# Attention on one core: the order and the step size in which the SP queue brings queries, masks and the last stage's inputs

## The chip, the cores and the metric

The kernel runs on one core of a Trainium2 chip. A core has a matrix engine (PE), a vector engine (DVE), an activation engine (ACT), a general engine (POOL), and a sequencer (SP) that in this kernel issues the DMA transfers. Each engine has its own instruction stream and runs it in order; streams meet at semaphores. The metric is the device time of one execution in microseconds (us), less is better. It is the median of several runs.

## The reference, cut to what matters

Two graph attention layers and one transformer layer over 4096 nodes with 256 features, all sharing one 4096 x 4096 adjacency matrix. The change lies in the transformer layer. It has 8 heads of 32 features each:

```
qkv = layer_norm(x, g1, be1) @ w_qkv
q, k, v = split of qkv into 8 heads of 32
scores = (q . k) * 32**-0.5           # 8 x 4096 x 4096
scores = where(adj != 0, scores, -inf)
attn = softmax(scores)
x = x + (attn @ v) @ w_proj + b_proj
x = x + gelu(layer_norm(x, g2, be2) @ w1 + b1) @ w2 + b2
```

## The kernel before, in words

The graph attention layers and the query, key and value products of the transformer come first and are not touched. Then `unshifted_transformer` (L1633) runs the attention stage and the last stage (projection, layer norm, two feed-forward products).

**The attention stage.** Queries are cut into 8 blocks of 512 (`nb`), heads into two quads of four (`c`), keys into 32 tiles of 128 (`mt`). One `(nb, c, mt)` is a unit; there are 512 units, and each is done in two halves (`u`), each for two heads. `weights` (L1810) does a half: eight PE matmuls (L1819) write scores into a PSUM tile `u_ps` of 128 x 1024 numbers (three such buffers), ACT takes the exponential in place (L1826), DVE multiplies by the mask into `u_e` (L1828). PE later multiplies `u_e` with the values (`weigh`, tile `u_av`) and sums it with a column of ones (`total`, tile `u_dn`), both by `four` (L1834). For seven pairs of units out of eight, POOL adds two `u_e` first (`u_both`, L1946), so that PE sums one tile and not two; the eighth pair (`alone`, L1856) is summed tile by tile. These PE pieces wait in a list and are put behind the scores of later halves, three or four per half. At the end of a quad ACT copies both sums out (L1853, L1870), they are stored to DRAM, and two late steps reload and invert the sums (`quad_end`, L1867).

**What has to be loaded.** A block needs its queries (`u_q`, four transfers of 256 KB, L1711; two buffers) and its mask (`u_mask`, four chunks of 512 KB for eight key tiles each, L1723; five buffers). Keys and values of all tiles stay in SBUF. `load_early` (L1887) brings, in quad 1 of the last block, all weights of the last stage (`wp`, `bp`, `b2`, `w1`, `w2`) and the rows, attention sums and inverted sums of its first two blocks, into space of the keys of quad 0 (`u_k0`, no longer used by then), one `u_q` buffer and one mask buffer: some 5.5 MB. POOL adds the bias to those rows and multiplies the sums with the inverses (L1960, L1963).

**What sets the order.** Inside the attention stage PE, ACT and DVE keep the order of the program text (`manual_schedule`, L1931 and L1932). SP and POOL are not in that set: the planner of the framework places their instructions when, by its own reckoning, inputs and buffers are ready. So transfers go out when a buffer comes free and not where the text has them. In the stage before (query, key and value products) SP does keep the order of the text, and there too `load_queries(0)` and `load_chunk(0, ..)` are called. In the last stage only PE keeps the order of the text. Order between engines is kept by semaphores in every case.

Of the kernel before, what the change touches and what calls it, by code (L numbers as in the profile page):

```python
# [8 lines left out]
F32 = mybir.dt.float32  # L9
BF = mybir.dt.bfloat16  # L10
F16 = mybir.dt.float16
# [3 lines left out]
U8 = mybir.dt.uint8  # L15
# [7 lines left out]
P = 128  # L23
# [695 lines left out]
def spread(src, ap):  # L719

    return bass.AP(tensor=src.tensor, offset=src.offset, ap=ap)
# [9 lines left out]
class Rows:  # L731
# [5 lines left out]
    def load(self, to, at, cols=slice(None)):  # L737

        end = at + to.shape[1]
        for block, start, n in zip(self.blocks, block_starts(self.tiles), self.tiles):  # L740
            a, b = max(at, start), min(end, start + n)
            if a < b:
                self.nc.sync.dma_start(
                    to[:, a - at : b - at, :],
                    block[(a - start) * P : (b - start) * P, cols].rearrange(
                        "(t p) d -> p t d", p=P
                    ),
                )
# [884 lines left out]
def unshifted_transformer(  # L1633
# [22 lines left out]
    nc = tc.nc  # L1656
    N, D = out.shape
    DC = D // P
    F = w1.shape[1]
    FC = F // P  # L1660
    NT = N // P
    NB = 512
    NNB = N // NB
# [21 lines left out]
    masks = ctx.enter_context(tc.tile_pool(name="u_masks", bufs=5))  # L1685


    def load_rows(nb, res, att, inv):
        rows.load(res, nb * TB)
        nc.sync.dma_start(att, att_d[:, :, nb * NB : (nb + 1) * NB].rearrange("c p n -> p c n"))  # L1690
        for j in range(HC):
            nc.sync.dma_start(
                inv[j * O : (j + 1) * O],
                spread(inv_d[nb * DC, j : j + 1, :], [[0, O], [HC * NB, DC], [1, NB]]),
            )

    with ExitStack() as scope:
# [7 lines left out]
        def stack(to, i, order, cols, c, heads):  # L1705

            for a, kind in enumerate(order):
                if kind is None:
                    continue
                first = half_d[i, kind, c, 0:1, cols]  # L1710
                nc.sync.dma_start(  # L1711
                    to[a * O : (a + 1) * O],
                    spread(first, [[N, O], [O * N, heads], [1, NB]]),
                )

        def load_queries(nb):
            q_st = blocks.tile([P, DC * HC, NB], F16, name="u_q")
            stack(q_st, 0, (0, 1, 0, 1), slice(nb * NB, (nb + 1) * NB), 0, DC * HC)
            block_tiles[nb] = q_st, []

        def load_chunk(nb, k):
            b = masks.tile([P, MC, NB], U8, name="u_mask")
            nc.sync.dma_start(  # L1723
                b.rearrange("p (c m) n -> p c (m n)", c=2),
                mask_d[nb][2 * k : 2 * k + 2].rearrange("c p n -> p c n"),
            )
            block_tiles[nb][1].append(b)

        with ExitStack() as qkv:
            hv = qkv.enter_context(tc.tile_pool(name="u_hv", bufs=3))  # L1730
# [79 lines left out]
        def weights(nb, c, mt, u):  # L1810

            q_st, chunks = block_tiles[nb]
            mask = chunks[mt // MC][:, mt % MC, :].unsqueeze(1).to_broadcast([P, 2, NB])
            ps = ps_s.tile([P, 2, NB], F32, name="u_ps")
            for j in range(2):
                h = c * HC + 2 * u + j
                for r in range(HC):
                    at = mt * P + r * O
                    nc.tensor.matmul(  # L1819
                        ps[r * O : (r + 1) * O, j, :],  # L1820
                        k_st[c][:, 2 * u + j, at : at + O],
                        q_st[:, h, :],
                        start=True,
                        stop=True,
                    )
            nc.scalar.activation(ps, ps, AF.Exp, scale=SCALE)  # L1826
            e = work.tile([P, 2, NB], F32, name="u_e")
            nc.vector.scalar_tensor_tensor(e, mask, 0.0, ps, op0=ALU.not_equal, op1=ALU.mult)  # L1828
            return e
# [57 lines left out]
        def load_early():  # L1887

            slab = slab_p.tile([P, 32 * D], F32, name="u_k0")
            at = 0  # L1890

            def piece(n, pattern, **dims):
                nonlocal at
                at += n * D
                return slab[:, at - n * D : at].rearrange(pattern, **dims)

            early["wp"] = piece(DC, "p (c e) -> p c e", c=DC)
            nc.sync.dma_start(early["wp"], w_proj.rearrange("(c p) e -> p c e", p=P))
            for name, src in (("bp", b_proj), ("b2", b2)):
                early[name] = piece(1, "p (o e) -> p o e", o=1)  # L1900
                nc.sync.dma_start(early[name][:, 0], spread(src, [[0, P], [1, D]]))
            two = blocks.tile([P, 2, TB * D], F32, name="u_q")
            early[0] = (
                piece(TB, "p (t d) -> p t d", t=TB),
                piece(TB, "p (c n) -> p c n", c=DC),
                piece(TB, "p (c n) -> p c n", c=DC),
            )
            early[1] = (
                two[:, 0].rearrange("p (t d) -> p t d", t=TB),
                two[:, 1].rearrange("p (c n) -> p c n", c=DC),  # L1910
                masks.tile([P, DC, NB], F32, name="u_mask"),
            )
            for nb in range(2):
                load_rows(nb, *early[nb])
            early["w1"] = piece(FC, "p (c f) -> p c f", c=DC)
            nc.sync.dma_start(early["w1"], w1.rearrange("(c p) f -> p c f", p=P))
            early["w2"] = piece(FC, "p (f e) -> p f e", f=FC)
            nc.sync.dma_start(early["w2"], w2.rearrange("(c p) e -> p c e", p=P))

        early = {}  # L1920
        units = [(nb, c, mt) for nb in range(NNB) for c in range(DC) for mt in range(NT)]
# [6 lines left out]
                [lambda part=part: step(*units[i], es, part) for part in range(PARTS)]  # L1928
            )

        ordered = {mybir.EngineType.PE, mybir.EngineType.Activation, mybir.EngineType.DVE}  # L1931
        scope.enter_context(tc.manual_schedule(engines=ordered))  # L1932
        for i in range(len(units) + 5):
            for u in range(HC // 2):
                if i < len(units):
                    nb, c, mt = units[i]
                    if u == 0 and c == DC - 1 and mt % MC == 2 and nb + 1 < NNB:
                        if mt < MC:
                            load_queries(nb + 1)
                        load_chunk(nb + 1, mt // MC)  # L1940
                    if u == 0 and units[i] == (NNB - 1, DC - 1, 4):
                        load_early()
                    es_of.setdefault(i, []).append(weights(*units[i], u))
                    if i % 2 == 1 and not alone(mt):
                        both = work.tile([P, 2, NB], F32, name="u_both", bufs=6)
                        nc.gpsimd.tensor_tensor(both, es_of[i - 1][u], es_of[i][u], op=ALU.add)  # L1946
                        both_of.setdefault(i, []).append(both)
                if u == 0 and 0 <= i - 2 < len(units):
                    ready(weigh, i - 2, es_of[i - 2])
                if u == 1 and i - 4 in both_of:  # L1950
                    ready(total, i - 4, both_of.pop(i - 4))
                if u == 1 and 0 <= i - 2 < len(units) and alone(units[i - 2][2]):
                    ready(total, i - 2, es_of[i - 2])
                count = AFTER[i % 2 * 2 + u] + (len(waiting) > 3 * PARTS)
                for _ in range(min(count, len(waiting))):
                    waiting.pop(0)()
            for k, unit in enumerate(((NNB - 1, DC - 1, NT // 2 - 1), units[-1])):
                if i < len(units) and units[i] == unit:
                    res, att, inv = early[k]
                    nc.gpsimd.tensor_tensor(  # L1960
                        res, res, early["bp"].to_broadcast([P, TB, D]), op=ALU.add
                    )
                    nc.gpsimd.tensor_tensor(att, att, inv, op=ALU.mult)  # L1963
            if i == len(units) - 1:
                nc.scalar.activation(rooted, norms.eps, AF.Sqrt)
            if i % 2 == 0 and later:
                later.pop(0)()
        assert not waiting
        while later:
            later.pop(0)()  # L1970

# [1 line left out]
    with ExitStack() as scope:  # L1973
# [7 lines left out]
        def rows_of(nb):  # L1981
            res = tail.tile([P, TB, D], F32, name="u_xres", bufs=4)
            att = tail.tile([P, DC, NB], F32, name="u_att")
            inv = tail.tile([P, DC, NB], F32, name="u_wide")
            load_rows(nb, res, att, inv)
            nc.gpsimd.tensor_tensor(res, res, bp_sb, op=ALU.add)
            nc.vector.tensor_tensor(att, att, inv, op=ALU.mult)
            return res, att
# [186 lines left out]
```

## Time and profile before

| what | value |
|---|---|
| median of 3 runs | 3158.15 us (3156.18 to 3162.9) |
| the profiled execution: its own time | 3161.47 us |
| its span, first to last instruction | 3159.7 us |
| granted clock of PE over the span | 0.994 |
| attention stage, from the first scores to the last mask product | about 1700.6 to 2891.1 us |
| last stage | about 2895 us to the end |
| busy shares over the span: PE, DVE, ACT, POOL | 98%, 88%, 85%, 38% |

Times in the profile are in us from the start of the span, those of single instructions in ns where marked. An instruction group is named by its line, its engine, its operation and its tiles (out<-in). In a timeline, the bracket at the end of a line says how long the engine sat idle before it and what ended that; "issue" stands for idle time in which it waited for nothing that the profile shows. In a table of stretches, each engine has its busy time and, in brackets, its count of instructions; then follow the granted PE clock, the mean busy share of the 16 DMA engines and GB/s. DMA queues are named by number; "instruction" is the kind of the packets that bring the engines' own programs.

### The profile page before, as it was taken

To read this page: it belongs to the slowest core of one execution; us is meant where nothing else is said; L and a number is where in the kernel's file an instruction comes from. 1 tells how busy PE (TensorE), PEld (TensorE's weight loads), DVE (VectorE), ACT (ScalarE), POOL (GpSimd) and SP (SyncE) were. 2 spreads that over 40 slices of the span, in tenths; PEclk is the share of its full clock that TensorE was granted. 3 is DMA by queue.
4 is the path that set the end of the run, shared out by engine and by line. 5 is a ranking of instruction groups with operands and counts; after the bars stand their busy time and mean duration, and the time that the engine had idled before them with its cause. 6 is when DMAs were issued, how large, how long until landed. Compare 5 with 4: busy or idle time off the path is not lost. (4 is left out here: it accounts for less than half of the span.)

```text
span 3159.7 us, 138934 instructions
## 1 busy us (share of the span) xinstructions
PE 3084.4 (98%) x63976; PEld 2715.3 (86%) x63976; DVE 2786.5 (88%) x3140; ACT 2682.1 (85%) x3228; POOL 1196.6 (38%) x538
## 2 busy tenths in 40 slices
PE   6999999999999999999998999999999999999998
PEld 5899999999889999999975888888878888877766
DVE  7999999999889999999976999999999999998221
ACT  6899999999899999999965888888888888886232
POOL 3300000000320000000003988898988888997110
PEclk8999999999999999999999999999999999999999
DMA  7666554420311213121145010101011010121210
GB/s 259 220 201 197 166 190 149 151 86 23 112 44 39 79 56 96 42 67 38 46 127 158 14 41 21 34 21 34 28 27 39 18 49 8 48 61 56 70 34 22
DMA packets 212034, 250.33 MB, mean 79 GB/s; under 512 B 88241, under 2 KB 132785, under 8 KB 211441
## 3 DMA queue, kind: packets, MB, share of 16 engines
q1 hardware_dynamic: 211440, 241.36, 24.9%
q8 instruction: 502, 8.22, 1.1%
q14 instruction: 92, 0.75, 0.1%
HBM read 198.84 MB, written 42.47 MB: 76 GB/s over the span
## 5 line engine op out<-in xcount | busy, mean ns | idle before, releaser
L1462 PE MATMUL bank<-vst,t 128*128 128x132 f16 x16384 | 1457.3, 220 | 9.7 <-DVE t L1137 9.5
L1946 POOL TENSOR_TENSOR u_both<-u_e 128x1024 f32<-128x1024 f32 x448 | 1049.7, 2385 | 902.8 <-DMA u_k<-half_d 782.8
L1462 PE MATMUL bank<-vst,mask 128*128 128x132 f16 (+1 forms) x10516 | 1372.4, 206 | 0.0
L1122 ACT ACTIVATE t<-s_b,g_terms 128x1024 int8<-128x1024 f32 x1234 | 1320.8, 1162 | 24.3 <-PE bank L1462 18.9
L1462 PEld LDWEIGHTS <-t 128*128 128x128 fp8e4 x16384 | 1186.4, 96 | 22.9 <-DVE t L1137 12.5
L1828 DVE SCALAR_TENSOR_TENSOR u_e<-u_mask,u_ps 128x1024 f32<-128x1024 uint8 x1024 | 1165.9, 1220 | 23.7 <-ACT u_ps L1826 20.6
L1826 ACT ACTIVATE u_ps<-u_ps 128x1024 f32<-128x1024 f32 x1024 | 1030.0, 1008 | 147.4 <-PE u_ps L1819 49.4
L1462 PEld LDWEIGHTS <-mask 128*128 128x128 fp8e4 x10516 | 920.7, 98 | 0.0
L1137 DVE SCALAR_TENSOR_TENSOR t<-mask,t 128x2048 int32<-128x2048 int32 x256 | 588.5, 2299 | 74.8 <-ACT t L1122 66.5
L1819 PE MATMUL u_ps<-u_q,u_k 128*32 128x512 f16 x8192 | 642.6, 383 | 11.0 <-issue 7.3
L1837 PE MATMUL u_av<-u_e,u_v 128*32 128x128 f32 x16384 | 605.7, 273 | 2.6 <-issue 2.6
L1837 PEld LDWEIGHTS u_av<-u_e,u_v 128*32 128x32 f32 x16384 | 492.0, 110 | 131.5 <-issue 5.2
L1124 DVE TENSOR_SCALAR t<-s_b,g_terms 128x1024 fp8e4<-128x1024 f32 x814 | 591.0, 758 | 2.4 <-DMA s_b<-s_d 2.4
L1054 POOL TENSOR_TENSOR vst<-g_adj,vst 128x528 f16<-128x528 f32 x16 | 19.8, 1239 | 727.2 <-ACT g_big L1018 682.7
L1837 PE MATMUL u_dn<-u_both,u_ones 128*32 128x128 f32 x7168 | 281.9, 273 | 1.6 <-issue 1.6
L1819 PEld LDWEIGHTS <-u_k 128*32 128x32 f16 x8192 | 231.4, 95 | 58.6 <-issue 17.9
L1837 PEld LDWEIGHTS u_dn<-u_both,u_ones 128*32 128x32 f32 x7168 | 213.7, 110 | 41.9 <-issue 2.1
L2041 ACT ACTIVATE u_hid<-misc,n_b 128x512 f32<-128x512 f32 x64 | 43.9, 687 | 140.2 <-PE misc L2034 140.1
L2054 PE MATMUL misc<-u_k,u_hid 128*128 128x256 f32 x512 | 111.8, 379 | 0.0
L2034 PE MATMUL misc<-ln_cols,u_k 128*128 128x512 f32 x256 | 111.3, 592 | 0.5 <-ACT ln_cols L1558 0.5
L2054 PEld LDWEIGHTS misc<-u_k,u_hid 128*128 128x128 f32 x512 | 96.7, 190 | 13.3 <-issue 0.5
L2034 PEld LDWEIGHTS misc<-ln_cols,u_k 128*128 128x128 f32 x256 | 48.6, 190 | 58.5 <-issue 56.9
(171 smaller groups left out, 1808.9 us busy)
## 6 DMA issues: line engine op xcount, KB each, us to landing
g_adj<-in_adj_dram SPq DMA_DIRECT2D x123, 512.0 KB
s_b<-s_d SPq DMA_DIRECT2D x64, 512.0 KB
mask<-mask SPq DMA_DIRECT2D x128, 256.0 KB
u_mask<-mask SPq DMA_DIRECT2D x32, 512.0 KB
mask<-stage SPq DMA_DIRECT2D x48, 256.0 KB
half_d<-u_halves SPq DMA_DIRECT2D x32, 256.0 KB
u_q<-half_d SPq DMA_DIRECT2D x32, 256.0 KB
rows<-e_x SPq DMA_DIRECT2D x31, 256.0 KB
```

The costliest lines, as they stand in the source:

```text
L1122: nc.scalar.activation(to.bitcast(I8), s, AF.Sign, bias=negd, scale=-1.0)
L1124: nc.vector.tensor_scalar(to, s, negd, -1.0, op0=ALU.is_ge, op1=ALU.mult, saturate=False)
L1137: nc.vector.scalar_tensor_tensor(both, m32.unsqueeze(1).to_broadcast(list(both.shape)), SIGNS, both, op0=ALU.bitwise_or, op1=ALU.bitwise_and,)
L1462: nc.tensor.matmul(to, left, right, start=k not in opened, stop=last)
L1819: nc.tensor.matmul(ps[r * O : (r + 1) * O, j, :], k_st[c][:, 2 * u + j, at : at + O], q_st[:, h, :], start=True, stop=True,)
L1826: nc.scalar.activation(ps, ps, AF.Exp, scale=SCALE)
L1828: nc.vector.scalar_tensor_tensor(e, mask, 0.0, ps, op0=ALU.not_equal, op1=ALU.mult)
L1837: nc.tensor.matmul(to[j * O : (j + 1) * O, at], lefts[j], es[j // 2][:, j % 2, at], start=first and part == 0, stop=last and part == PARTS ...
L1946: nc.gpsimd.tensor_tensor(both, es_of[i - 1][u], es_of[i][u], op=ALU.add)
L2034: nc.tensor.matmul(ph, w1_sb[:, k, f * P : (f + 1) * P], hn[:, k, :], start=(k == 0), stop=(k == DC - 1),)
L2041: nc.scalar.activation(hid[:, f, :], ph, AF.Gelu_apprx_tanh, bias=norms.sb["b1"][:, f : f + 1])
L2054: nc.tensor.matmul(po[:, :D], hid[:, f, at : at + P], w2_sb[:, f, :], start=(f == 0), stop=(f == FC - 1),)
```

## The change

Three things change, all inside `unshifted_transformer`.

1. SP joins the set of engines that keep the order of the text in the attention stage.
2. Transfers are cut. A mask chunk of 512 KB becomes two of 256 KB. The early rows, sums and inverses go by half or by feature chunk, `w1` in four pieces of 256 KB, `wp` in two and `w2` in eight of 128 KB. Queries keep their four transfers of 256 KB.
3. A list `pacing` holds such steps. At the start of every unit `pace` takes at most one: it has ACT copy one column (`norms.eps`, 128 x 1 or 32 x 1) into the first column of the step's target, and then issues the transfer, which overwrites it. The transfer writes the same place, so it has to wait for the copy, and the copy stands in ACT's order before the unit's first exponential. The queries of block `nb + 1` enter the list at quad 0, tile 20 (four steps), the halves of mask chunk `k` at quad 1, tile `8k + 2` (two steps each), the early loads at the last block's quad 1, tile 4 (28 steps, for the 28 units that are left).

The loads of the stage before the attention (`load_queries(0)`, `load_chunk(0, ..)`) use the same steps without the copy, all at once.

```diff
+    def row_steps(nb, res, att, inv):
+        def sums(c):
+            nc.sync.dma_start(att[:, c], att_d[c, :, nb * NB : (nb + 1) * NB])
+        def inverses(c):
+            for j in range(HC):
+                nc.sync.dma_start(
+                    inv[j * O : (j + 1) * O, c],
+                    spread(inv_d[nb * DC + c, j : j + 1, :], [[0, O], [1, NB]]),
+                )
+        h = TB // 2
+        steps = [
+            (res[:, k : k + h], lambda k=k: rows.load(res[:, k : k + h], nb * TB + k))
+            for k in (0, h)
+        ]
+        for c in range(DC):
+            steps.append((att[:, c : c + 1], lambda c=c: sums(c)))
+            steps.append((inv[:, c : c + 1], lambda c=c: inverses(c)))
+        return steps
...
+        pacing = []
+        def pace():
+            if pacing:
+                (to, eps), load = pacing.pop(0)
+                nc.scalar.copy(to, eps)
+                load()
+        def query_steps(nb):
+            q_st = blocks.tile([P, DC * HC, NB], F16, name="u_q")
+            block_tiles[nb] = q_st, []
+            cols = slice(nb * NB, (nb + 1) * NB)
+            return [
+                (
+                    (q_st[a * O : (a + 1) * O, 0, :1], norms.eps[a * O : (a + 1) * O]),
+                    lambda a=a, kind=kind: stack(
+                        q_st, 0, [kind if k == a else None for k in range(HC)], cols, 0, DC * HC
+                    ),
+                )
+                for a, kind in enumerate((0, 1, 0, 1))
+            ]
...
+        def chunk_steps(nb, k):
+            b = masks.tile([P, MC, NB], U8, name="u_mask")
+            block_tiles[nb][1].append(b)
+            m = MC // 2
+            def part(c):
+                nc.sync.dma_start(
+                    b[:, m * c : m * (c + 1)].rearrange("p m n -> p (m n)"), mask_d[nb][2 * k + c]
+                )
+            return [((b[:, m * c, :1], norms.eps), lambda c=c: part(c)) for c in range(2)]
...
-            for nb in range(2):
-                load_rows(nb, *early[nb])
-            early["w1"] = piece(FC, "p (c f) -> p c f", c=DC)
-            nc.sync.dma_start(early["w1"], w1.rearrange("(c p) f -> p c f", p=P))
...
+            def add(to, load):
+                pacing.append(((to[:, 0, :1], norms.eps), load))
...
+            vector("bp", b_proj)
+            rows_of(0)
+            rows_of(1)
+            for c in range(DC):
+                matrix("wp", w_proj, c, slice(0, D))
+            for half in range(2):
+                for c in range(DC):
+                    matrix("w1", w1, c, slice(half * F // 2, (half + 1) * F // 2))
+            vector("b2", b2)
+            for f in range(FC):
+                matrix("w2", w2, f, slice(0, D))
...
-        ordered = {mybir.EngineType.PE, mybir.EngineType.Activation, mybir.EngineType.DVE}
+        ordered = {
+            mybir.EngineType.PE, mybir.EngineType.Activation, mybir.EngineType.DVE,
+            mybir.EngineType.SP,
+        }
...
-                    if u == 0 and c == DC - 1 and mt % MC == 2 and nb + 1 < NNB:
-                        if mt < MC:
-                            load_queries(nb + 1)
-                        load_chunk(nb + 1, mt // MC)
+                    if u == 0 and nb + 1 < NNB:
+                        if c == 0 and mt == 20:
+                            pacing.extend(query_steps(nb + 1))
+                        if c == DC - 1 and mt % MC == 2:
+                            pacing.extend(chunk_steps(nb + 1, mt // MC))
                     if u == 0 and units[i] == (NNB - 1, DC - 1, 4):
                         load_early()
+                    if u == 0:
+                        pace()
```

More of the change, by code (lines that the diff above doesn't have):

```diff
@@ L1714, in stack @@
                 )
-        def load_queries(nb):
-            q_st = blocks.tile([P, DC * HC, NB], F16, name="u_q")
-            stack(q_st, 0, (0, 1, 0, 1), slice(nb * NB, (nb + 1) * NB), 0, DC * HC)
-            block_tiles[nb] = q_st, []
-        def load_chunk(nb, k):
[L1722 to L1727, printed above, removed]
+        pacing = []
[17 more added lines that the diff above has]
+            ]
+        def load_queries(nb):
+            for _, load in query_steps(nb):
+                load()
+        def chunk_steps(nb, k):
[7 more added lines that the diff above has]
+            return [((b[:, m * c, :1], norms.eps), lambda c=c: part(c)) for c in range(2)]
+        def load_chunk(nb, k):
+            for _, load in chunk_steps(nb, k):
+                load()
         with ExitStack() as qkv:
@@ L1897, in load_early @@
             early["wp"] = piece(DC, "p (c e) -> p c e", c=DC)
[L1898 to L1902, printed above, removed]
+            early["bp"], early["b2"] = (piece(1, "p (o e) -> p o e", o=1) for _ in range(2))
             early[0] = (
@@ L1907, in load_early @@
             )
+            early["w1"] = piece(FC, "p (c f) -> p c f", c=DC)
+            early["w2"] = piece(FC, "p (f e) -> p f e", f=FC)
+            two = blocks.tile([P, 2, TB * D], F32, name="u_q")
             early[1] = (
@@ L1912, in load_early, with vector, rows_of, matrix @@
             )
-            for nb in range(2):
-                load_rows(nb, *early[nb])
-            early["w1"] = piece(FC, "p (c f) -> p c f", c=DC)
-            nc.sync.dma_start(early["w1"], w1.rearrange("(c p) f -> p c f", p=P))
-            early["w2"] = piece(FC, "p (f e) -> p f e", f=FC)
-            nc.sync.dma_start(early["w2"], w2.rearrange("(c p) e -> p c e", p=P))
+            def add(to, load):
+                pacing.append(((to[:, 0, :1], norms.eps), load))
+            def vector(name, src):
+                to = early[name]
+                add(to, lambda: nc.sync.dma_start(to[:, 0], spread(src, [[0, P], [1, D]])))
+            def rows_of(nb):
+                for load in row_steps(nb, *early[nb]):
+                    add(*load)
+            def matrix(name, src, c, cols):
+                to = early[name][:, c : c + 1, cols]
+                at = src[c * P : (c + 1) * P, cols]
+                add(to, lambda: nc.sync.dma_start(to[:, 0], at))
+            vector("bp", b_proj)
[9 more added lines that the diff above has]
+                matrix("w2", w2, f, slice(0, D))
         early = {}
@@ L1967, in unshifted_transformer @@
                 later.pop(0)()
-        assert not waiting
+        assert not waiting and not pacing
         while later:
```

## The prediction, made before the change was run

> **What bounds the kernel now.** I read the page first (PE is busy 98% of the span, so only lost PE time or a second engine near its limit can matter), then the groups of instructions, then the attention stage in stretches, then PE's and DVE's timelines at each place where a stretch fell short. The groups, with each engine's operation in the attention stage:
>
> ```profile
> L1946 POOL TENSOR_TENSOR u_both<-u_e 128x1024 f32<-128x1024 f32 x448 | 1049.7, 2385 | 902.8 <-DMA u_k<-half_d 782.8
> L1828 DVE SCALAR_TENSOR_TENSOR u_e<-u_mask,u_ps 128x1024 f32<-128x1024 uint8 x1024 | 1165.9, 1220 | 23.7 <-ACT u_ps L1826 20.6
> L1826 ACT ACTIVATE u_ps<-u_ps 128x1024 f32<-128x1024 f32 x1024 | 1030.0, 1008 | 147.4 <-PE u_ps L1819 49.4
> ```
>
> DVE has 1024 mask products and 24 us of idle time before them; ACT has 147 us. So DVE, not ACT, stands beside PE as a limit. DVE's timeline in an undisturbed part:
>
> ```profile
> 2035.29 37.70 DVE L1828 SCALAR_TENSOR_TENSOR u_e<-u_mask,u_ps 128x1024 f32<-128x1024 uint8 x33
> ```
>
> 33 products follow each other without a gap: (37.70 - 1.22) / 32 = 1.14 us apart; the densest runs in the timeline are 1.13 apart. PE's score groups are 1.09 apart at their fastest and 1.3 in four halves of each 32, where four pieces of sums follow the scores instead of three. DVE sets the pace, and PE for a few halves. Now stretches around the places with loss (times of PE, PEld, DVE, ACT, POOL, then clock, DMA share, GB/s):
>
> ```profile
> 1713.00:1719.00 6.00, 5.67 (x148) 4.00 (x141) 6.00 (x6) 5.63 (x6) 5.11 (x4) 1.00 1.11 206
> 1719.00:1722.00 3.00, 0.30 (x4) 0.16 (x7) 1.78 (x2) 0.11 (x1) 3.00 (x2) 0.96 0.36 115
> 2001.00:2007.00 6.00, 6.00 (x184) 4.92 (x180) 6.00 (x6) 5.21 (x6) 2.31 (x2) 1.00 0.90 178
> 2007.00:2012.00 5.00, 4.40 (x129) 3.55 (x121) 4.01 (x4) 3.64 (x5) 4.37 (x2) 1.00 0.30 95
> 2822.00:2831.00 9.00, 6.41 (x186) 5.62 (x178) 6.71 (x6) 5.83 (x7) 9.00 (x5) 1.00 0.97 302
> ```
>
> Each loss of PE comes during or just after a stretch with the DMA engines full. PE's timeline at the three places, and what SP had issued before them:
>
> ```profile
> 1721.70 0.61 PE L1819 MATMUL u_ps<-u_q,u_k 128*32 128x512 f16 x4 [2.73 <-issue]
> 2009.49 0.40 PE L1819 MATMUL u_ps<-u_q,u_k 128*32 128x512 f16 x3 [0.60 <-issue]
> 2824.49 0.53 PE L1837 MATMUL u_av<-u_e,u_v 128*32 128x128 f32 x11 [2.03 <-issue]
> ```
> ```profile
> 1710.49 1.91 SPq L1711 DMA_DIRECT2D u_q<-half_d  x4
> 1712.45 0.45 SPq L1723 DMA_DIRECT2D u_mask<-mask  x1
> 2000.51 1.82 SPq L1711 DMA_DIRECT2D u_q<-half_d  x4
> ```
>
> PE stops in the middle of a group of eight and waits for nothing that another engine does. The trace's packets say why: one instruction queue brings 16 KB every 4.45 us in this stage, once per 256 PE instructions. The packet due at 2004.4, while the 1 MB of queries (2001.7 to 2006.5) was moving, began at 2006.8; the one due at 1713.7 began at 1719.3; the one due near 2819, in the early loads, at 2821.6. Delays of 1.0 to 1.3 us, behind single mask chunks of 512 KB, stopped nothing; 2.4 us cost 0.6. So PE tolerates some 1.8 us.
>
> **What the skill says.** Runtime: NRT & Kernel Launch, "Instruction fetch mechanics": each sequencer fetches blocks of 16 KiB, 256 instructions, over its own DMA queue while it executes the one before, and the cost is "mostly hidden". The trace agrees on block and count and shows where it is not hidden. DMA: Bandwidth & Descriptors, "Queues, rings and completion order": each DMA engine takes turns between its rows packet by packet; so a fetch should wait for little of a burst, yet it waited 2.4 of the 4.8 us that the queries moved. The measurement decides.
>
> **What it removes.** I took DVE's start of every 32nd mask product (16 units) from the timeline. Undisturbed cycles last 36.48 us; one in which a quad ends, 36.87 (two more ACT copies of 0.59). The table is of the others:
>
> | cycle | us | against | excess |
> |---|---|---|---|
> | the first | 41.48 | halves 12 to 14: 3.83 + 2.20 + 1.50 for 3 x 1.13 | 4.14 |
> | starts of blocks 1 to 6 | 37.83, 37.84, 37.57, 37.88, 38.03, 38.01 | 36.87 | 5.94 |
> | last block, quad 1, early loads | 39.64 | 36.87 | 2.77 |
>
> Sum 12.85 us. The start of block 7, which has no queries to load behind it, is the control: 36.87. After the change queries go in four parts of 256 KB, one per unit of 2.28 us, in the middle of quad 0. 1 MB moved in 4.8 us, so a part moves in 1.2 us and a fetch can wait 1.2 us, under the 1.8 tolerated. The same for 256 KB of anything else (a 512 KB chunk landed 3.2 us after its issue and stopped nothing). At the stage's start 4.2 MB moved from 1700 to 1720.5; 1.57 MB of it were block 1's queries and a mask chunk. Without these the packets of the trace reach the same count by 1712.9, just before the fetch due at 1713.7. Hence all three rows should go.
>
> **What it adds.** 7 x (4 + 8) + 28 = 112 ACT copies. The nearest row is the one 128 x 1 ACT operation on `n_eps` (L1965): 205 ns. ScalarE: Activation LUTs, "What ACT_TABLE_LOAD costs", gives 186 ns plus 0.833 per element, and 93 ns of overlap between neighbours; in the trace a 1.01 us exponential at 2007.65 has its successor at 2008.57, an overlap of 0.09. So exponential and copy take 0.92 + 0.12 = 1.04 us, under the 1.09 in which PE can deliver: the copy fills ACT's wait for PE. Cover gone means 0.12 us each. It is gone where a quad has just ended and ACT also has its 0.59 us copies (tiles 2 and 3 of quad 1, tiles 4 and 5 in the last block): 16 copies, 1.9 us at most. Queries at tiles 20 to 23 meet DVE with 0.05 to 0.35 us of slack: next to nothing. Bounds for all: 0 and 112 x 0.205 = 23 us. I take 1.5.
>
> Behind a waiting copy stand the unit's exponentials, so its waits matter: buffers. Chunk k of the next block takes the buffer of chunk k - 1, last read at tile 8k - 1, and is copied into at 8k + 2, with DVE about one half behind ACT; `u_q` was last read a whole quad ago; the slab's last reader is PE, four units ago. All are past.
>
> SP in text order: a transfer can now stand behind the store of sums, and the reload of the denominators behind that store's landing (2.2 us after issue at 1790.79). DVE's reciprocal that needs it comes two units later (4.6 us) and today has 3.5 us to spare; a step in front costs it 1.2. Nothing. The added issues (about 0.4 us each) are on an idle SP. In the last stage, rows of block 2 are issued from 2894.84 on; if all came after the last inverse store (2905.43), six issues, 1.5 MB and one DVE product end near 2916, and PE takes them at 2917.92. Nothing, with 2 us to spare.
>
> POOL's four early operations (2.4 us each) move with their loads. From both timelines, POOL's sums are ready 3.5 to 4.7 us before PE takes them; three of those operations in one run of pairs ate all of it today, helped by PE's 2.6 us stop. Now two or three fall in tiles 7 to 14 and perhaps one after tile 17: 0 to 2 us, I take 1.
>
> 12.85 - 1.5 - 1 = 10.35 us. The profiled execution would go from 3161.47 to 3151.1 (span 3149.3); the median, 3.3 below that execution, from 3158.15 to 3147.8.
>
> **Rivals.** (1) Half the gain: the fetch at the start still meets the key loads (4.1 lost), or POOL and copies take their upper ends (2 more). For it: the drain at 1712.9 leaves 0.8 us before the fetch. It gives 3151 to 3156, say 3153. (2) No change: other bursts hit the fetches instead; 28 units in a row now carry a step of 128 to 256 KB, some 110 GB/s. Against it: 27 mask chunks of 512 KB, each alone, hit none. 3156 to 3161. (3) Slower: the copy of a step waits for the transfer of the step before, because both write one tile (76 such steps: 21 of queries, 28 of masks, 27 early). The first query part landed 3.4 us after its issue and the next copy is due after 2.28, so ACT would lose up to 1.1 and I take 0.7 each: 53 - 13 = +40, about 3198. It decides from 0.17 us per step. Against it: PE read `u_k` at 1700.64 with sixteen transfers into the same tiles still to be issued (1700.88 on), so waits go by place and not by tile.
>
> **How the numbers follow.** All stalls gone, 0.62: 3144 to 3151, point 3147.8. Half the gain 0.18, no change 0.10, slower 0.10. A measurement of this kernel can tell about 0.2% (6.3 us) from no change: below 3151.8 lie the first and a quarter of the second (0.66), above 3164.5 the last (0.10), the rest 0.24. The range 3143 to 3159 holds the first two and half of the third.
>
> **What would show it.** PE's waits with "issue" in the attention stage fall from 9.1 us (from 1705 on) to under 2; block starts take 36.9 us per cycle, the first cycle about 37.3; queries leave SP in fours 2.3 us apart. The copies show as 112 ACT rows near 0.2 us with no DVE idle behind them. Wrong if a copy's row has idle time before it ended by a DMA, if DVE's idle time before L1828 grows over 24 us, or if a fetch still starts late.

## The result, and the profile after

| | before | after |
|---|---|---|
| median of 15 runs each | 3158.15 us (3155.12 to 3162.9) | 3150.14 us (3148.41 to 3152.85) |
| profiled execution, its own time (span) | 3161.47 us (3159.7) | 3150.14 us (3148.4) |
| ratio of the medians | | 0.9974, 95% interval 0.9967 to 0.9981 |

The kernel became faster by 8.0 us. The prediction had 3147.8 for the median, so the sign is right and the gain came out 2.3 us smaller than forecast. The profiled execution went to 3150.14 where 3151.1 was forecast. Those two errors have opposite signs, and that is the first thing to explain below.

The groups of the attention stage in the profile of after (POOL's pair sums, DVE's mask products, ACT's exponentials, and the ACT copies that the change adds):

```profile
L2025 POOL TENSOR_TENSOR u_both<-u_e 128x1024 f32<-128x1024 f32 x448 | 1049.5, 2388 | 896.9 <-DMA u_k<-half_d 780.7
L1880 DVE SCALAR_TENSOR_TENSOR u_e<-u_mask,u_ps 128x1024 f32<-128x1024 uint8 x1024 | 1164.6, 1207 | 13.3 <-ACT u_ps L1878 4.9
L1878 ACT ACTIVATE u_ps<-u_ps 128x1024 f32<-128x1024 f32 x1024 | 1029.8, 1008 | 125.0 <-PE u_ps L1871 36.0
L1744 ACT CAST u_mask<-n_eps 128x1 uint8<-128x1 f32 x56 | 10.6, 189 | 0.2
L1744 ACT CAST u_q<-n_eps 32x1 f16<-32x1 f32 x28 | 5.2, 187 | 0.5
L1744 ACT COPY u_k<-n_eps 128x1 f32<-128x1 f32 x22 | 4.1, 185 | 0.0
```

DVE's idle time fell from 23.7 to 13.3 us. The copies are there (56 + 28 + 22, and 6 more into `u_q` and `u_mask`: 112), each 0.18 to 0.19 us, and ACT was hardly idle before them, 0.7 us for all 112, so none of them waited for a transfer. SP's timeline of after shows the queries and the halves of mask chunks leaving in steps:

```profile
1747.89 6.96 SPq L1733 DMA_DIRECT2D u_q<-half_d  x4
1797.64 39.05 SPq L1771 DMA_DIRECT2D u_mask<-mask  x6
```

Four query transfers take 6.96 us to leave, one per unit; before, four left in 1.8 to 1.9 us. The stretches of after, with the columns of the prediction's table (PE, PEld, which is PE's loading of weights, DVE, ACT, POOL, clock, DMA share, GB/s):

```profile
1747.00:1757.00 10.00, 10.00 (x301) 8.19 (x293) 10.00 (x9) 9.50 (x14) 10.00 (x5) 1.00 0.38 109
2001.00:2007.00 6.00, 6.00 (x184) 4.94 (x178) 5.66 (x6) 5.82 (x8) 5.89 (x4) 1.00 0.14 51
2007.00:2012.00 5.00, 5.00 (x151) 3.96 (x147) 5.00 (x5) 4.38 (x6) 4.90 (x3) 1.00 0.03 7
2822.00:2831.00 9.00, 9.00 (x260) 7.08 (x256) 9.00 (x9) 8.41 (x13) 9.00 (x5) 1.00 0.57 158
2836.00:2848.00 12.00, 10.23 (x280) 7.92 (x272) 8.93 (x9) 8.41 (x12) 12.00 (x6) 1.00 0.30 83
```

The queries (first row) move at 109 GB/s and PE loses nothing. The block start at 2007 and the early loads at 2822 are whole. The last row is new: at 2836 to 2848 PE loses 1.8 us and DVE 3.1, with the DMA engines at a share of 0.30 and POOL busy throughout. This loss has another cause than DMA. PE's timeline of after at two places of it:

```profile
2839.47 0.30 PE L1889 MATMUL u_dn<-u_both,u_ones 128*32 128x128 f32 x2 [0.63 <-POOL u_both L2025]
2845.39 0.62 PE L1871 MATMUL u_ps<-u_q,u_k 128*32 128x512 f16 x8 [0.72 <-DVE u_e L1880]
```

and DVE's in the same stretch:

```profile
2839.45 3.48 DVE L1880 SCALAR_TENSOR_TENSOR u_e<-u_mask,u_ps 128x1024 f32<-128x1024 uint8 x3 [0.79 <-POOL u_both L2025]
2844.11 1.22 DVE L1880 SCALAR_TENSOR_TENSOR u_e<-u_mask,u_ps 128x1024 f32<-128x1024 uint8 x1 [1.18 <-POOL u_both L2025]
2846.43 32.88 DVE L1880 SCALAR_TENSOR_TENSOR u_e<-u_mask,u_ps 128x1024 f32<-128x1024 uint8 x29 [1.10 <-POOL u_both L2025]
```

DVE waits for POOL: a `u_e` buffer comes free only when POOL has read it into a pair sum. PE stands twice behind that, once for a late sum (`u_dn`), once because DVE in its turn has not freed a score tile.

**Where the time went.** As in the prediction, the stage is cut by the start of every 32nd mask product (a cycle of 16 units). "Stage start" is the time from the first score matmul to product 33, "last quad" from the first product of the last block's quad 1 to the start of the last product. Each row is one execution.

| kernel | stage start | cycles at the starts of blocks 1 to 6, over 36.87 | last quad |
|---|---|---|---|
| before, profiled execution | 45.69 | .96 .97 .70 1.01 1.16 1.14 = 5.94 | 74.99 |
| before again (e0) | 40.04 | .68 1.05 .65 .80 1.02 1.37 = 5.57 | 75.57 |
| before, third (e11) | 42.98 | .83 .96 1.07 .61 1.02 1.10 = 5.59 | 75.16 |
| after | 39.66 | none | 75.34 |
| e1 | 41.67 | none | 72.30 |

Three readings follow. The block starts are the steady part of the gain: 5.6 to 5.9 us, all of it gone. The stage start differs by 5.6 us between executions of one and the same kernel. And the last quad, where 2.77 us should have gone, did not get shorter at all.

### The profile page after: what moved, and what is told of

Read it like the earlier page. It is cut to its first block, busy times and chain, and to the rows that moved or that the text cites. A ratio compares the mean times of both kernels' runs of the same rounds, so it can differ in the third digit from the quotient of the medians.

```text
span 3148.4 us, 139188 instructions
## 1 busy us (share of the span) xinstructions
PE 3081.3 (98%) x63976; PEld 2708.4 (86%) x63976; DVE 2784.0 (88%) x3140; ACT 2690.9 (85%) x3340; POOL 1195.9 (38%) x538
## 4 chain that ended last, share of the span: by engine, by line
PE 47%; ACT 2%; DVE 2%; POOL 1%; issue 1%; DMA 0%; SPq 0%; DVEq 0%; ACTq 0%; POOLq 0%
PE u_ps L1871 15%; PE u_av L1889 14%; PE u_dn L1889 8%; PE misc L2133 4%; PE misc L2113 3%; ACT t L1122 2%; PE misc L1809 2%; POOL u_both L2025 1%; PE misc L2074 1%; PE misc L1828 1%; DVE t L1124 1%; DVE t L1137 1%; PE misc L1555 0%; DVE u_e L1880 0%; ACT ev_broad L1472 0%
## 5 line engine op out<-in xcount | busy, mean ns | idle before, releaser
L1880 DVE SCALAR_TENSOR_TENSOR u_e<-u_mask,u_ps 128x1024 f32<-128x1024 uint8 x1024 | 1164.6, 1207 | 13.3 <-ACT u_ps L1878 4.9
L1871 PE MATMUL u_ps<-u_q,u_k 128*32 128x512 f16 x8192 | 632.0, 382 | 6.8 <-DVE u_e L1880 4.3
L1889 PE MATMUL u_av<-u_e,u_v 128*32 128x128 f32 x16384 | 597.8, 273 | 0.0
L1889 PEld LDWEIGHTS u_av<-u_e,u_v 128*32 128x32 f32 x16384 | 483.4, 110 | 131.7 <-issue 0.6
L1871 PEld LDWEIGHTS <-u_k 128*32 128x32 f16 x8192 | 224.5, 95 | 53.2 <-issue 11.5
L2133 PEld LDWEIGHTS misc<-u_k,u_hid 128*128 128x128 f32 x512 | 96.7, 190 | 13.3 <-issue 0.5
```

The costliest lines, as they stand in the source:

```text
L1871: nc.tensor.matmul(ps[r * O : (r + 1) * O, j, :], k_st[c][:, 2 * u + j, at : at + O], q_st[:, h, :], start=True, stop=True,)
L1889: nc.tensor.matmul(to[j * O : (j + 1) * O, at], lefts[j], es[j // 2][:, j % 2, at], start=first and part == 0, stop=last and part == PARTS ...
L2133: nc.tensor.matmul(po[:, :D], hid[:, f, at : at + P], w2_sb[:, f, :], start=(f == 0), stop=(f == FC - 1),)
```

## The experiments

All kernels below compute the full reference. Each is an edit of after or of before, as its diff shows.

**e0 and e11: the kernel before, unchanged.** They ask which rows of the prediction's table belong to the kernel and which to the one execution that was read.

> The kernel before, profiled once more. Theory A: the queries behind a block's start meet the fetch due there every time, so the six block cycles again take 37.6 to 38.0 us, and the cycle with the early loads about 39.6. The first cycle (41.48 us) is the open one: the run without copies had the same burst at the stage's start and lost only about 1 us there. If the 41.48 comes back it belongs to the kernel; if it is 37 to 39 us, some 3 to 4 us of the difference between the two profiles, and not of the medians, were chance.

> The kernel before, unchanged, for a third look at its start. If the first cycle's 41.48 us belonged to the one profiled execution: 36.5 to 38 us here as in the second look (37.41), with block starts again at 37.5 to 38.2. If it is a property of the kernel: near 41.

Measured: 3155.22 and 3157.55 us. The block starts came back in both (5.57 and 5.59 us). The stage start did not. PE's timeline of e0 there:

```profile
1720.70 0.40 PE L1819 MATMUL u_ps<-u_q,u_k 128*32 128x512 f16 x4 [0.58 <-issue]
```

and that of e11:

```profile
1719.36 0.40 PE L1819 MATMUL u_ps<-u_q,u_k 128*32 128x512 f16 x4 [2.18 <-issue]
```

The stop of 2.73 us in the prediction's profile is 0.58 us in one execution and 2.18 in another. PE's waits put down to "issue" after 1705 us come to 9.1, 6.1 and 8.6 us in the three, and to none in after. So the first row is worth less: on the mean of three, the start takes (45.69 + 40.04 + 42.98) / 3 = 42.90, against 40.83 on the mean of the six kernels of this study without a query burst there (39.66 to 41.67; after, e1, e4, e5, e6, e8): 2.1 us. Two more kernels, e2 and e3 below, still have the burst at the start and take 45.42 and 41.07; with them the difference is 2.2. It is a rough figure, since e0 with the burst lies among those without it. The prediction read 4.14 from one execution, the slowest of the three.

**e6, e8, e9: the four query transfers at once, but in program order and behind a copy, at a chosen unit.** They ask whether the size of the burst or its moment stops PE.

```diff
-                            pacing.extend(query_steps(nb + 1))
+                            steps = query_steps(nb + 1)
+                            pacing.append((steps[0][0], lambda steps=steps: [load() for _, load in steps]))
```

e6 keeps `mt == 20`, e8 has `mt == 21`, e9 has `mt == (6, 1, 2, 3, 4, 18, 19)[nb]`.

> The changed kernel, with the four query transfers of a block behind one copy at quad 0, tile 20, at once (1 MB) and not one per unit. Same bytes, same transfers, away from the block's start. Theory A: the second cycle of quad 0 (36.47 us) takes 37 to 37.6 us in the blocks where a fetch falls into the burst, 0.6 to 1.2 us in each of 7 blocks, so 4 to 8 us in all: 3154 to 3158 us. Rival D (the loss before came from the change of block, not from the burst): 3150 us, all those cycles 36.47.

> The changed kernel with a block's four query transfers at once at quad 0, tile 21, one unit later than in the run with tile 20. A unit has 132 PE instructions and a fetch brings 256, so one unit shifts the burst by half a fetch interval. Theory A': a burst does harm only where it meets the start of a fetch: then PE stops for 0.5 to 1 us in each of 7 blocks, DVE loses what goes beyond 0.3 to 0.4 us, and the second cycle of quad 0 takes 36.7 to 37.2 us, 2 to 5 us in all. Rival D (bursts are harmless away from a block's start): no PE stop, all cycles 36.47, 3151 us.

> As before, with the burst of the seven blocks at quad 0 at tiles 6, 1, 2, 3, 4, 18 and 19. Theory A': neighbouring tiles give opposite phases, so in each pair (1, 2), (3, 4), (18, 19) one stops PE (0.5 to 1 us) and the other does not; in tiles 1 to 4, where DVE has no work in store, the whole stop is lost, elsewhere all but 0.3 to 0.4 us. Rival D (the block's start): tiles 1 and 2 lose 1 us both, the others nothing.

Measured: e6 3151.19 us, ratio to before 0.9976 (0.9968 to 0.9984), as good as after and not the 3154 to 3158 us of theory A. e8 3152.9 us, 0.9986 (0.9978 to 0.9995). e9 3153.12 in one run. In e6 no cycle with a burst is longer than the same cycle of after by more than 0.02 us. In e8, one unit later, four of seven blocks, and not all, lose 1.22, 0.48, 0.50 and 0.46 us. In e9 the bursts at tiles 1, 2, 3, 4 and 19 lose 0.40, 0.25, 1.44, 1.18 and 0.28 us, those at tile 6 and 18 nothing. So of the three neighbouring pairs only 18 and 19 behave in opposite ways, as was expected of all three. The stretches of e6 around the burst of the third block, issued at 2041.99:

```profile
2043.00:2049.00 6.00, 6.00 (x188) 5.11 (x184) 6.00 (x7) 5.56 (x6) 6.00 (x4) 1.00 0.80 177
2049.00:2055.00 6.00, 6.00 (x176) 4.69 (x171) 6.00 (x6) 5.49 (x6) 6.00 (x4) 1.00 0.01 3
```

The same stretches of e8, whose burst was issued at 2045.37:

```profile
2045.00:2051.00 6.00, 6.00 (x188) 5.05 (x183) 6.00 (x6) 5.61 (x8) 6.00 (x4) 1.00 0.81 164
2051.00:2057.00 6.00, 5.49 (x161) 4.73 (x153) 5.63 (x6) 4.78 (x5) 6.00 (x3) 1.00 0.09 16
```

And PE's timeline of e8 in the second of them, where it waits for nothing that another engine does:

```profile
2052.96 0.30 PE L1889 MATMUL u_dn<-u_both,u_ones 128*32 128x128 f32 x2 [0.51 <-issue]
```

Same bytes, same DMA share (0.80 and 0.81), and only the second stops PE. From the packets, with the spacing of 4.45 us for when a block is due (good to some 0.2 us): PE's instruction blocks were due 4.7 us after the burst's first issue in e6, 2.4 us in e8 and 3.7 us in before. They began 1.1 to 2.0 us late in e6 with no stop. In e8 four began 2.3 to 3.3 us late and stopped PE, three began 1.2 to 1.4 us late and did not. In before's block starts they were 1.8 to 2.6 us late and all stopped PE. So the cause named in the prediction holds, a late block of instructions, with a tolerance of about 1.8 to 2.0 us (between 1.8 and 2.0 both outcomes occur). A second reading of the packets agrees: the twelve traces have 43 stops of PE of 0.13 us or more in the attention stage, from 1705 us on, that are put down to "issue", and every one ends 2.3 to 2.9 us after the packet of a block began (1.2 to 1.6 us after it had moved), where chance would spread them over the whole 4.45 us between two blocks. What a burst does also depends on where it falls between two fetches. A block of queries takes 33 x 256 PE instructions, so the position repeats in every block; but it doesn't decide alone. Why in e8 three of seven fetches at the same position were late by only 1.2 to 1.4 us stays open.

The two largest losses of e9, at tiles 3 and 4, have another cause. DVE's timeline of e9 there:

```profile
2160.48 0.25 DVE L1931 RECIPROCAL u_inv<-u_dens 128x16 f32<-128x16 f32 x1 [1.35 <-DMA u_dens<-den_d]
2308.36 0.25 DVE L1931 RECIPROCAL u_inv<-u_dens 128x16 f32<-128x16 f32 x1 [1.03 <-DMA u_dens<-den_d]
```

These tiles are where the sums of the quad before are stored and reloaded. On SP the burst stands ahead of the store (tile 3) or of the reload (tile 4) of the denominators, and DVE waits for the reload. PE's stops there are put down to DVE, not to "issue". The same cause, far larger, comes back in e2.

The Trainium skill (Runtime: NRT & Kernel Launch, "Instruction fetch mechanics") speaks of PE holding 2048 instructions, and in the same section of two blocks of 256. A reserve of 2048 would last eight intervals of 4.45 us. These runs fit the two blocks and not the 2048: the tolerance of 1.8 to 2.0 us and the 2.3 to 2.9 us from a packet's start to the end of a stop make 4.1 to 4.9 us, so when a fetch is due PE has about one block, 4.45 us of work, in hand. That is an estimate from these figures.

**e2, e3, e5: order, cuts and copies apart.** e2 is before with SP in program order and nothing else. e3 is after without the copies. e5 is after with SP left to the planner.

```diff
 # e2, from before
-        ordered = {mybir.EngineType.PE, mybir.EngineType.Activation, mybir.EngineType.DVE}
+        ordered = {
+            mybir.EngineType.PE, mybir.EngineType.Activation, mybir.EngineType.DVE,
+            mybir.EngineType.SP,
+        }
 # e3, from after
-                nc.scalar.copy(to, eps)
 # e5, from after
-            mybir.EngineType.SP,
```

> SP in program order alone; nothing is cut, no copies. Each block's 1 MB of queries and a 512 KB mask chunk then leave SP together at quad 1, tile 2, and all early loads at quad 1, tile 4 of the last block. If the step size counts: block starts stay at 36.87 us, the cycle that begins at quad 1 (36.87 in after) grows by 0.4 to 1.4 us in most blocks, the last block's quad 1 stays near 75 to 76 us, and the median lies at 3153 to 3158. If the order alone counts: no such growth and a median within 2 us of 3150.

> The changed kernel without the ACT copies: same text order, same small transfers, but nothing holds a transfer back except its buffer and what stands before it on SP. Theory A: SP runs ahead, so queries, masks and early loads go out in bursts again, the first cycle is over 40 us, some block cycles 37.5 to 38 us, and the time is 3155 to 3160 us. Rival C (the order on SP and the smaller transfers bring the gain, the copies bring nothing): 3150 us, first cycle 37.1, block cycles 36.86.

> The changed kernel with SP taken out of the set of engines that keep the order of the text; copies and small transfers stay. Theory A: the copies alone hold the transfers back, 3149 to 3151 us, block cycles 36.86. Rival C (the order on SP matters): slower, over 3154 us.

Measured: e2 3171.79 us, ratio 1.0035 (1.002 to 1.0049), slower than before and outside of what was expected. e3 3155.64 us, 0.9989 (0.9981 to 0.9997). e5 3151.03 us, 0.9977 (0.9969 to 0.9985), the same as after.

e2 is the instructive one. The bursts do not leave at quad 1, tile 2, where the text has them and where they were expected. Block 1's queries leave at the stage's start (1707.87), and those of later blocks some 19 us after a block's first scores, right behind the store of the inverted sums that stands ahead of them on SP:

```profile
1869.77 0.34 SPq L1880 DMA_DIRECT2D inv_d<-u_inv  x1
1870.21 1.85 SPq L1711 DMA_DIRECT2D u_q<-half_d  x4
```

There they do less harm than at the block's start: four of the cycles at the starts of blocks 1 to 6 take 36.86 us, two lose 0.25 and 0.38. Then its last block's quad 1 takes 94.5 us where before has 75.0. SP's timeline of e2 there:

```profile
2815.83 1.12 SPq L1872 DMA_DIRECT2D den_d<-u_den  x4
2816.99 0.40 SPq L1898 DMA_DIRECT2D u_k<-in_L_gnn_w_proj_dram  x1
...
2830.31 0.43 SPq L1916 DMA_DIRECT2D u_k<-in_L_gnn_w_dram  x1
2831.55 0.39 SPq L1918 DMA_DIRECT2D u_k<-in_L_gnn_w_dram  x1
2833.99 1.75 SPq L1875 DMA_DIRECT2D u_dens<-den_d  x1
```

and DVE's at the end of its wait:

```profile
2843.93 0.25 DVE L1879 RECIPROCAL u_inv<-u_dens 128x16 f32<-128x16 f32 x1 [20.30 <-DMA u_dens<-den_d]
```

The text has the reload of the denominators (L1875) two units after their store, and the early loads between the two. In program order the reload stands behind all of them and is issued 17 us after the end of the store's four issues, and then waits for 5.5 MB already handed to the DMA engines. DVE reaches its reciprocal, which it must do in order, and stands still for 20.3 us, with all mask products that are left behind it in its queue. In after, the same order costs nothing, because at most one step stands in front: SP's timeline there has the reload between two steps.

```profile
2812.67 0.36 SPq L1970 DMA_DIRECT2D u_k<-in_L_gnn_b_proj_dram  x1
2813.47 0.34 SPq L1927 DMA_DIRECT2D u_dens<-den_d  x1
2813.91 1.99 SPq L743 DMA_DIRECT2D u_k<-rows  x2
```

e3 shows what the copies do. Without them a step may leave as soon as its buffer is free, even with SP in the order of the text:

```profile
1708.45 1.98 SPq L1733 DMA_DIRECT2D u_q<-half_d  x4
1866.79 1.86 SPq L1733 DMA_DIRECT2D u_q<-half_d  x4
```

The bursts are back (1.98 and 1.86 us for four), one of them in the stage's start. The time is within what theory A had, though the first cycle, 38.58 us, is not over 40. Against after, e3's stage is 4.8 us longer (1179.93 against 1175.16 from the first to the last product): 2.2 in the last quad, 1.5 in the first cycle, 0.8 in cycles with queries. With the copies and SP free (e5) nothing is lost. So with the transfers cut, the copies bring the whole gain, and SP's place in the ordered set adds nothing measurable to them. Order and cuts without the copies bring a part: e3 is 2.9 us under the kernel before measured beside it (3158.55 us), e5 7.5 us. No run has the copies with all transfers uncut, so what the cuts are worth alone is not shown; for the queries, e6 shows no loss without them.

**e1: POOL in program order too.**

```diff
-            mybir.EngineType.SP,
+            mybir.EngineType.SP, mybir.EngineType.Pool,
```

> The changed kernel with POOL, too, in the order of the text in the attention stage, so that the four early POOL operations stand after tile 15 and after the last tile of the last quad. Theory A (bursts held up the instruction fetch; what the early loads gained was given back because the four POOL operations fell among the sums of pairs): the last two cycles of 16 units go from 37.8 and 37.5 us to 36.9 and 35.4, the idle time of DVE behind POOL (3.2 us) goes to about zero, and the time is 3147 us, 3 us under the changed kernel. Rival B (the ACT copies or the 28 transfers in a row slow the last quad): nothing changes, 3150 us.

Measured: 3147.9 us (3145.31 to 3149.07), ratio 0.9969 (0.9957 to 0.9981). It is what theory A had (3147), and the fastest kernel of the study; measured beside e5 and e6, its 6 runs lie below all 13 of e5, and only one of the 14 of e6 (3148.59) is under its highest. POOL's timeline of after in the last quad (what is left out is pair sums):

```profile
2820.68 2.40 POOL L2039 TENSOR_TENSOR u_k<-u_k 128x1024 f32<-128x1024 f32 x1
...
2832.36 2.40 POOL L2042 TENSOR_TENSOR u_k<-u_k 128x1024 f32<-128x1024 f32 x1
...
2839.35 2.40 POOL L2039 TENSOR_TENSOR u_q<-u_q,u_k 128x1024 f32<-128x1024 f32 x1
...
2846.34 2.40 POOL L2042 TENSOR_TENSOR u_q<-u_q,u_mask 128x1024 f32<-128x1024 f32 x1
```

and that of e1:

```profile
2818.34 23.41 POOL L2025 TENSOR_TENSOR u_both<-u_e 128x1024 f32<-128x1024 f32 x10 [0.19 <-DVE u_e L1880]
2841.70 2.37 POOL L2039 TENSOR_TENSOR u_k<-u_k 128x1024 f32<-128x1024 f32 x1
2844.03 2.38 POOL L2042 TENSOR_TENSOR u_k<-u_k 128x1024 f32<-128x1024 f32 x1
2846.38 32.73 POOL L2025 TENSOR_TENSOR u_both<-u_e 128x1024 f32<-128x1024 f32 x14
2879.07 2.38 POOL L2039 TENSOR_TENSOR u_q<-u_q,u_k 128x1024 f32<-128x1024 f32 x1
```

In after the planner puts all four operations into 28 us, between pair sums, as soon as their loads have landed. A quad holds 28 sums of 2.34 us in some 73 us, so POOL has about 8 us to spare in a whole quad, mostly in two gaps at its `alone` pairs, one in the middle and one at the end. In after three of the four operations, 7.2 us, stand before the first 14 sums of the quad are done, and so before the first gap. In the text the first two stand at the gap in the middle, the last two behind the last sum, and e1 keeps them there. DVE's waits for POOL (3.2 us in after; 3.1 to 3.2 in e5, e6, e8 and e9 too) are gone from its list of waits, and the last quad takes 72.30 us instead of 75.34: 3.0 us. That is the price of POOL's step in after.

**e4: each step's copy four times.**

```diff
-                nc.scalar.copy(to, eps)
+                for _ in range(4):
+                    nc.scalar.copy(to, eps)
```

> The changed kernel with four ACT copies per step instead of one: 336 more. If a copy costs 0.12 us of ACT and hides in ACT's wait for PE, a unit takes ACT 1.84 + 0.48 = 2.3 us against 2.26 that DVE takes, so it is at the edge: 0 to 4 us more than the changed kernel, 3150 to 3154 us. If a copy costs its full 0.2 us: 0.24 us more per paced unit and more where sums end, 27 us or more, 3177 us.

Measured: 3184.34 us, ratio 1.0085 (1.0071 to 1.0099), above the 3177 of the second expectation ("27 us or more"), and far from the first. ACT's timeline of e4 at query steps:

```profile
2203.69 0.87 ACT L1745 CAST u_q<-n_eps 32x1 f16<-32x1 f32 x4
2204.47 1.90 ACT L1879 ACTIVATE u_ps<-u_ps 128x1024 f32<-128x1024 f32 x2
2206.39 0.85 ACT L1745 CAST u_q<-n_eps 32x1 f16<-32x1 f32 x4
```

and DVE's:

```profile
2205.57 2.35 DVE L1881 SCALAR_TENSOR_TENSOR u_e<-u_mask,u_ps 128x1024 f32<-128x1024 uint8 x2 [0.41 <-ACT u_ps L1879]
```

With four copies a unit of ACT takes 2206.39 - 2203.69 = 2.70 us, and DVE, which needs 2.28 us for a unit, waits 0.41. The copies do not overlap one another (0.85 / 4 = 0.21 us each), though the last overlaps the exponential behind it. Two exponentials take 1.90 us, so ACT has 0.38 us per unit. One copy, which delays the next exponential by 0.10 us in after (2194.04 to 2194.14, below), fits; by this arithmetic two would fit and three would not. ACT's timeline of after at such a step:

```profile
2194.04 0.19 ACT L1744 CAST u_q<-n_eps 32x1 f16<-32x1 f32 x1
2194.14 12.16 ACT L1878 ACTIVATE u_ps<-u_ps 128x1024 f32<-128x1024 f32 x11
```

The cycles of e4 give the sum: a cycle with query steps lasts 38.35 against 36.48, the two with mask steps 38.03 and 37.24 against 36.87 and 36.48, in all 7 x (1.87 + 1.16 + 0.76) = 26.5, and the last quad 6.3, together 32.8 of the 33.2 us by which e4's stage is longer than after's. In after, the same cycles with single copies last 36.48, 36.87 and 36.48, which is what they last in before, without copies.

## Why the prediction was right, point by point

**The bound and the mechanism.** PE stopping for its own instructions behind DMA bursts was the right cause: every stop put down to "issue" after 1705 us is gone in after, and a burst put back at a chosen tile brings the stops back at some tiles (e8, e9). DVE's pace of 1.14 us per half and the 36.87 us of an undisturbed block start held to 0.01 us.

**The terms of the sum**, in us:

| term | predicted | measured | from |
|---|---|---|---|
| stage start | +4.14 | +2.1 on the mean of three executions | before, e0, e11 against six kernels without the burst |
| starts of blocks 1 to 6 | +5.94 | +5.7 on the same mean | cycles |
| early loads | +2.77 | +2.9 | mean last quad of before, 75.24, less e1's 72.30 |
| ACT copies | -1.5 | 0.0 | cycles of after, e4 |
| POOL's four operations | -1 | -3.0 | after against e1 |
| sum | 10.35 | 7.7 | medians: 8.0 |

The point lies only 2.3 us from the measured median by some luck: the gain at the start was put 2.0 us too high and POOL's price 2.0 too low, which both make the forecast too fast, and the 1.5 us put down for copies that cost nothing took part of it back. Without that term it would have been 3.8 us off.

**The step that was mis-sized most against its own bounds is POOL's.** The prediction said that "two or three fall in tiles 7 to 14" and took 1 us from a range of 0 to 2. It looked at PE only: at when PE needs the sums. DVE is bound to POOL as well, through the `u_e` buffers that POOL must read before DVE may write them, and DVE had no reserve of its own (33 products in a row without a gap were quoted for that). The price, 3.0 us, lies outside of the bounds given, and it ate the whole gain of the early loads. The places were forecast well; what was missing is that three operations, 7.2 us, come before POOL's first gap. Against the 3.5 to 4.7 us by which the prediction saw the sums run ahead of PE, that would have given 2.5 to 3.7 us. This is an estimate, and takes for granted that DVE's reserve is about as large as PE's, which no run shows.

**The stage start** was read off one execution and applied to the median. The prediction knew that this execution was 3.3 us above its median and carried the difference through as if it were spread over the run. Part of it sat in the very row that was to vanish, so the profiled executions differ by 11.3 us and the medians by 8.0. That is why the forecast for the profile came out 1.0 too high and for the median 2.3 too low.

**The copies** were called hidden by ACT's wait for PE, with 1.5 us for places where the cover is gone. Nothing was paid there either. The cover is real and thin: 0.38 us per unit (e4).

**SP in text order at no cost** was right, and for the reason given, a single step in front of the reload. e2 prices what the prediction put aside: with the early loads uncut in front, the same order costs 20 us. At tiles 3 and 4 of e9 a burst of queries in front costs 1.44 and 1.18.

**The rivals.** Half the gain (3151 to 3156) had a true part: POOL's upper end was even passed, though the start did not stay lost. No change, because bursts of 128 to 256 KB hit the fetches instead, is excluded by after: the latest instruction block there began 1.7 us late, and none stopped PE. That is more than the 1.2 us that the prediction allowed for a step, and not far from the tolerance. Slower, because copies wait for the transfer into the same tile, did not happen; the idle time before all 112 copies comes to 0.7 us.

## What to carry to other kernels

An engine that runs dense code needs its instruction blocks on time; when it stops with "issue" in the profile, look at what the DMA engines carried in the few microseconds before, and give large loads that are not urgent a place and a rate, by an operation on an engine that has slack at that place. Program order alone binds nothing to a moment and can put an urgent small transfer behind a large one. When work of a nearly full engine is moved, look for everyone who waits for it, through its results and through the buffers that it frees, and take a loss read from one execution as a sample until a second one shows it again.

## What was not expected of the hardware

A burst of 1 MB cost nothing in seven blocks at tile 20 and up to 1.2 us in four of seven at tile 21: 2.3 us in time can decide, where an instruction block is due every 4.45 us and the burst moves for about 4.8. Part of a stop in PE can be taken up by the work queued between PE and DVE. Counted as idle time of PE's weight loads, which is 0.78 us where PE's line above has 0.51, stops of 0.78, 0.81 and 0.87 us in e8 cost DVE 0.48, 0.50 and 0.46 us. At before's block starts, stops of 0.70 to 1.14 us cost 0.70 to 1.16, so nothing was taken up there.
